# Probabilities of two self attentions turned by VectorE in 32 by 32 blocks

## The chip, the core and the metric

The kernel runs on one core of a Trainium2 chip. A core has five engines, each with an instruction queue of its own that is worked off in order: TensorE (matrix products and transposes, results in PSUM), VectorE, ScalarE, GpSimd and SyncE (here only a queue for DMA). The lines of the profile call them PE, with PEld for its weight loads, then DVE, ACT, POOL and SP. PSUM has 8 banks of 512 fp32 columns by 128 partitions. The metric is the device time of one execution in microseconds; less is better. All data are fp32.

## The reference

Two decoder layers act on x of shape (8 batches, 112 tokens, 512). Each layer is a self attention, a cross attention to a context of 375 rows of 128, and a feed-forward block, each on the layer norm of x and added to x. The two self attentions are what the change touches:

```
layer 0:  32 query heads, 8 key/value heads, width 64
          q, k, v = x@Wq+bq, x@Wk+bk, x@Wv+bv;  q, k rotated by position
          scores  = q.k / 8,  -inf where key > query or query - key >= 64
          probs   = softmax over [scores, sink of the head], sink column dropped
          out     = (probs @ v) @ Wo + bo
layer 1:  16 query heads, 4 key/value heads, width 128
          the same without biases, sinks, with a mask that hides
          nothing at 112 tokens
```

So a query of layer 0 sees the 64 keys up to itself, and a query of layer 1 sees all 112 keys. Layer 1's cross attention (16 heads of width 32, first 112 rows of the context, causal) uses the same softmax helper.

## The kernel before

Tokens lie on partitions where rows are normalised or added (x: seven tiles of 128 tokens), and on columns where they are multiplied (xT: two halves of 448 tokens, four batches each). A self attention (`self_attention`, line 434) has 8 turns: a turn is one group g of four (two key/value heads of layer 0, one of layer 1) and one half hf of the batches. A turn has units: four in layer 0 (a batch with two key/value heads), two in layer 1 (two batches with one key/value head). So every unit is 8 score matrices of 112 by 112.

For a unit, `scores` (line 575) makes the 8 matrices in a PSUM tile "s" of two banks (L583), and `softmax` (line 358) turns them into probabilities: mask added by VectorE in layer 0 (L366), negated row maximum by VectorE (L369), eight exponentials with row sums by ScalarE (L372), the reciprocal by VectorE (L375), and the product with it by GpSimd (L377). In layer 0 GpSimd also copies the sinks into a 113th column (L364). Queries are on the partitions of the result p; the product with v needs keys there. So `contexts` (line 590) begins with `probs_transposed` (line 380): TensorE transposes the 8 matrices, four into one bank of tag "t" (L388), and VectorE copies each bank to pT in SBUF (L389). Then `add` multiplies: v is the stationary operand, four transposed matrices side by side are the 448 moving columns (L599). In layer 0 the two key/value heads of a unit write the partitions 0 to 63 and 64 to 127 of one bank; in layer 1 the two batches write a bank each. ScalarE copies the result to oT (L604).

Around this lie the projections. `prepare(n)` makes keys and queries of turn n (`roped`, line 511): a product on TensorE (pr_k, pr_q), a copy by ScalarE, a DMA from SBUF to SBUF that exchanges halves (L527), a multiplication by VectorE (L530), two operations of GpSimd (L529, L531). `outputs(n, late)` multiplies finished tokens by Wo (po_at) and VectorE adds the result to x (`project_out`, L352). PSUM is shared by three tags of two buffers each: "mm" (projections, values, and po), "s" (scores, two banks each) and "t" (transposes).

TensorE's order is written out by hand. `pipeline` (line 394) gives for every unit: scores of the unit `ahead` (two in layer 0, one in layer 1), the two transposes' steps and `add`; with between=True (layer 0) the transposes come ahead of those scores. `weave` (line 237) spreads the fillers (the next turn's `prepare`, the finished `outputs`) between these steps in proportion to the costs noted beside them; a step marked True wants at least one filler ahead of it. The order of the other engines' queues is set by the framework's planner, from readiness in its own estimate of times and, among the ready, the order of the program. `tc.issue_after` ties some instructions behind another one; `copied` and `spread` hold the last copy and the last product of the softmax for it.

Two further places use these helpers: layer 1's cross attention (lines 1120 to 1249) calls `softmax` and `probs_transposed`, and `cross_attention_0` (line 722) ties the rotation of its context (lines 714 to 718) behind `copied`.

Of the kernel before, what the change touches and what calls it, by code (L numbers as in the profile page):

```python
# [15 lines left out]
P = 128  # L16
# [139 lines left out]
def decoder(ctx: ExitStack, tc: tile.TileContext, i: dict, out: bass.AP):  # L156
# [198 lines left out]
    def completed(hf, late):  # L355
        return [[[0], [1, 2]], [[3, 4], [5, 6]]][hf][late]

    def softmax(pool, ps, mask, sinks, name, bufs=3):

        n = T if sinks is None else T + 1  # L360
        p = pool.tile([T, 8, n], F32, tag="p", bufs=bufs, name=f"p_{name}")
        src = ps[:T, :, :T]
        if sinks is not None:
            nc.gpsimd.tensor_copy(p[:, :, T], sinks)  # L364
        if mask is not None:
            nc.vector.tensor_tensor(p[:, :, :T], src, mask.unsqueeze(1).to_broadcast([T, 8, T]), ALU.add)  # L366
# [10 lines left out]
        spread[:] = [nc.gpsimd.tensor_tensor(p[:, :, :T], p[:, :, :T], total, ALU.mult).ins]  # L377
        return p

    def probs_transposed(pool, p, kept, name):  # L380


        def turn(k):
            if k == 0:
                kept["pT"] = pool.tile([T, 8, T], F32, tag="pT", name=f"pT_{name}")
            pt = turning(f"ppt_{name}_{k}").rearrange("p (h t) -> p h t", h=4)
            for h in range(4):
                nc.tensor.transpose(pt[:T, h, :T], p()[:, 4 * k + h, :T], ident[:T, :T])  # L388
            copied[:] = [nc.vector.tensor_copy(kept["pT"][:, 4 * k : 4 * k + 4, :], pt[:T, :, :T]).ins]  # L389

        return [(0.45, lambda: turn(0)), (0.45, lambda: turn(1))]


    def pipeline(turns, units, ahead, prepare, scores, contexts, outputs, extra, begun=None, finale=None, between=False):

        queue = [(n, u) for n in range(len(turns)) for u in range(units)]  # L400

        def scored(k):
            return [(1.2, lambda: scores(*queue[k]))] if k < len(queue) else []

        def mains(n, us):
            steps = []
            for u in us:
                coming, own = scored(n * units + u + ahead), contexts(n, u)
                if between:
                    steps += own[:2] + coming + own[2:]  # L410
                else:
                    steps += coming + own
            return steps

        if begun is None:
            run(prepare(0) + extra(-1)[:1])
            weave([(1.0, step, True) for k in range(ahead) for _, step in scored(k)], extra(-1)[1:])
        for k in range(begun or (ahead if begun is None else 0), ahead):
            run(scored(k))
        end = len(turns) - 1  # L420
        for n in range(end + (finale is None)):
            filler, late = prepare(n + 1) if n < end else [], outputs(n - 1, True) if n else []
            weave(mains(n, range(units - ahead)), filler + late)
            weave(mains(n, range(units - ahead, units)), outputs(n, False) + extra(n))
        if finale is None:
            run(outputs(end, True))
        else:
            fillers, after = finale(outputs(end - 1, True) + outputs(end, False) + outputs(end, True))
            for u, filler in enumerate(fillers):
                weave(mains(end, [u]), filler)  # L430
            after()


    def self_attention(layer, following=None, behind=None, xT=None):
# [4 lines left out]
        half = width // 2  # L439
        turns = [(g, hf) for g in range(G) for hf in range(2)]  # L440
        held, matrices = [{} for _ in turns], {}

        if l0:
            pool, mid, top, tpool = (
# [29 lines left out]
        v = pool.tile([T, NB, D], F32, tag="v", bufs=1, name=f"v{layer}")  # L474

        oT = None

        def values(b):
            ps = mm(f"pv{layer}_{b}")
# [95 lines left out]
        def scores(n, u):  # L575
            g, hf = turns[n]
            nm = f"{layer}_{g}_{hf}_{u}"
            kT, qT = held[n]["kT"], held[n]["qT"]
            ps = wide(f"ps_{nm}").rearrange("p a (h k) -> p (a h) k", h=4)
            for h in range(4):  # L580
                for k, (b, s) in enumerate(parts(n, u)):
                    at = slice(s * width, (s + 1) * width)
                    nc.tensor.matmul(  # L583
                        ps[:T, 4 * k + h, :T], qT[at, h, bcols(b)], kT[at, bcols(b)], start=True, stop=True
                    )
            held[n]["p", u] = softmax(
                mid, ps, const("mask0", T) if l0 else None, row("sinks")[:, 8 * g : 8 * g + 8] if l0 else None, nm
            )

        def contexts(n, u):  # L590
            g, hf = turns[n]
            nm = f"{layer}_{g}_{hf}_{u}"
            kept = {}

            def add():
                po = [mm(f"po_{nm}_{k}") for k in range(1 if l0 else 2)]
                for k, (b, s) in enumerate(parts(n, u)):
                    at, kv = slice(s * width, (s + 1) * width), g * (P // width) + s
                    nc.tensor.matmul(  # L599
                        po[0 if l0 else k][at, :HT], v[:, b, kv * width : (kv + 1) * width],  # L600
                        kept["pT"][:, 4 * k : 4 * k + 4, :].rearrange("p h q -> p (h q)"), start=True, stop=True,
                    )
# [28 lines left out]
        def go():  # L631
            nonlocal oT, late
            if not l0:
                late = stage_pool("atl1")
                joined.append(following(npool, late))
            oT = (pool if l0 else late).tile([P, 4, NB * T], F32, tag="oT", bufs=1, name=f"oT{layer}")
            pipeline(
                turns, HB if l0 else HB // 2, 2 if l0 else 1, prepare, scores, contexts, outputs, extra,
                begun=None if l0 else 0, finale=finale, between=l0,
            )  # L640
            if l0:
                pool.release()
# [475 lines left out]
    def cross_attention_1(npool, tpool):  # L1118
# [90 lines left out]
        def scores(n, u):  # L1209
            b, nm = n * HB + u // 2, f"e_{n}_{u}"  # L1210
            ps = wide(f"ps_{nm}").rearrange("p a (h k) -> p (a h) k", h=4)
            for c in range(4):
                for k in range(2):
# [250 lines left out]
```

## Time and profile before

| | |
|---|---|
| median of 3 runs | 1901.36 us (1899.02 to 1903.3) |
| profiled execution | 1903.46 us |
| its span, first to last instruction | 1901.5 us |
| mean granted TensorE clock | 0.992 |
| TensorE busy | 1830.2 us (96%), 7088 matmuls |
| VectorE busy | 797.0 us (42%), 1391 instructions |
| ScalarE busy | 660.7 us (35%) |
| GpSimd busy | 585.5 us (31%) |
| stretch 97 to 400 us (seven eighths of layer 0's self attention) | TensorE 289.8, VectorE 174.3, ScalarE 125.2, GpSimd 143.6 of 303 us |
| stretch 1024 to 1166 us (four turns of layer 1's) | TensorE 141.9, VectorE 44.7, ScalarE 41.1, GpSimd 58.6 of 142 us |

How to read the lines: a group has line, engine, operation, the tile written and the tiles read, the shapes (for a matmul contraction * stationary columns, then partitions x moving columns), the count, then busy time in us and the mean of one in ns, then the idle time of the engine just before these instructions and what ended it. An fp32 matrix product is two matmul instructions, so counts are twice those of the code, except for transposes. In a timeline a line is a start, a duration and a run of like instructions; an idle time before it is in brackets. In a table by stretch the bracketed numbers count instructions, and after the busy times of the engines stand the granted clock, the share of the DMA engines and GB/s.

### The profile page before, as it was taken

What the parts mean: (1) busy time and instruction counts of PE and PEld (TensorE: products, weight loads), DVE (VectorE), ACT (ScalarE), POOL (GpSimd) and SP (SyncE); (2) the same over time, 40 slices, a digit from 0 to 9 for tenths busy, and PEclk for the clock granted to TensorE, in tenths of its full rate; (3) what the DMA queues carried; (4) which work ended last, traced back from release to release, by engine and by line L of the source; (5) the groups of instructions that cost most, each with busy time, mean ns of one, the idle gap of its engine ahead of it and who ended that gap; (6) DMA issues with size and microseconds to landing.
All of it is one profiled execution on the core that took longest, in us unless ns stands there. A gap on an engine that the chain in (4) does not pass through costs nothing.

```text
span 1901.5 us, 19724 instructions
## 1 busy us (share of the span) xinstructions
PE 1830.2 (96%) x7088; PEld 986.3 (52%) x7088; DVE 797.0 (42%) x1391; ACT 660.7 (35%) x1948; POOL 585.5 (31%) x512
## 2 busy tenths in 40 slices
PE   7999999899999999989999999999999999999999
PEld 4454544455454455557655555545555444554444
DVE  4455556645454544776532333336722112211213
ACT  3344433444333333375332232236722111121110
POOL 3454544245555540000034334302321111011111
PEclk9999999999999999999999999999999999999999
DMA  6132322243223212011221221301020000000001
GB/s 232 25 113 74 124 75 59 79 141 98 67 78 111 56 39 89 23 67 45 77 63 37 67 77 41 132 4 44 4 107 1 1 0 0 0 0 1 0 0 39
DMA packets 35497, 108.68 MB, mean 57 GB/s; under 512 B 6644, under 2 KB 20012, under 8 KB 28744
## 3 DMA queue, kind: packets, MB, share of 16 engines
q1 hardware_dynamic: 28264, 77.97, 12.7%
q0 software_dynamic: 6848, 29.36, 5.2%
q8 instruction: 56, 0.92, 0.2%
q14 instruction: 41, 0.34, 0.1%
q10 hardware_dynamic: 288, 0.09, 0.0%
HBM read 78.83 MB, written 10.22 MB: 47 GB/s over the span
## 4 chain that ended last, share of the span: by engine, by line
PE 84%; DVE 7%; ACT 5%; DMA 1%; POOL 1%; issue 1%; SPq 1%; ACTq 0%; DVEq 0%; POOLq 0%
PE pf L235 15%; PE po L235 10%; PE po_at L235 9%; PE pr_q L235 8%; PE po_x L235 5%; PE po_x L811 4%; PE pr_k L235 3%; PE pv L235 2%; PE pq_x L235 2%; PE ps L583 2%; PE ph L235 2%; PE po L599 2%; PE ps_x L777 2%; PE po_ff L1051 2%; PE ppt_x L802 2%; PE pk_x L756 2%
## 5 line engine op out<-in xcount | busy, mean ns | idle before, releaser
L235 PE MATMUL pr_q<-xT_at,wq 128*128 128x448 f32 x512 | 205.4, 546 | 2.0 <-ACT raw_q L522 2.0
L235 PE MATMUL po_at<-wo,oT 128*128 128x512 f32 x448 | 205.1, 603 | 0.5 <-ACT oT L604 0.5
L235 PE MATMUL pf<-xT_ff,fup 128*128 128x448 f32 x512 | 199.8, 541 | 1.6 <-ACT xT_ff L313 1.6
L1378 POOL TENSOR_TENSOR h<-silu,h 128x448 f32<-128x448 f32 x64 | 72.9, 1138 | 407.2 <-ACT silu L1377 407.2
L235 PE MATMUL po<-fdn,h 128*128 128x512 f32 x448 | 197.1, 592 | 0.0
L235 PEld LDWEIGHTS pf<-xT_ff,fup 128*128 128x128 f32 x512 | 96.0, 190 | 93.0 <-issue 87.2
L377 POOL TENSOR_TENSOR p<-p,total 112x896 f32<-112x896 f32 x48 | 82.4, 1718 | 192.1 <-DVE total L375 162.3
L235 PEld LDWEIGHTS pr_q<-xT_at,wq 128*128 128x128 f32 x512 | 94.4, 191 | 88.3 <-issue 77.5
L1361 ACT ACTIVATE h<-pf,cols 128x448 f32<-128x448 f32 x64 | 40.5, 633 | 280.5 <-PE pf L235 278.0
L235 PEld LDWEIGHTS po<-fdn,h 128*128 128x128 f32 x448 | 84.6, 190 | 100.7 <-issue 100.1
L372 ACT ACTIVATE p<-p,nmax 112x113 f32<-112x113 f32 x256 | 95.8, 376 | 114.5 <-DVE nmax L369 113.8
L235 PEld LDWEIGHTS po_at<-wo,oT 128*128 128x128 f32 x448 | 82.1, 191 | 94.1 <-issue 86.6
L235 PE MATMUL po_x<-vo,xoT 128*128 128x512 f32 x224 | 102.0, 598 | 0.6 <-ACT xoT L815 0.6
L235 PE MATMUL pf<-h,sw 128*128 128x448 f32 x256 | 101.5, 540 | 0.0
L811 PE MATMUL po_x<-pT_x,kv 125*128 125x448 f32 x192 | 89.3, 548 | 2.7 <-DVE pT_x L806 1.6
L389 DVE COPY pT<-ppt 112x448 f32<-112x448 f32 x96 | 57.3, 614 | 82.2 <-PE ppt L388 82.2
L783 DVE TENSOR_REDUCE nmax_x<-ps_x 112x2 f32<-112x750 f32 x64 | 57.1, 932 | 82.3 <-PE ps_x L777 81.9
L529 POOL TENSOR_TENSOR qT<-raw_q,consts 128x448 f32<-128x448 f32 x64 | 81.2, 1272 | 33.6 <-ACT raw_q L520 18.7
L531 POOL TENSOR_TENSOR qT<-qT,turned_q 128x448 f32<-128x448 f32 x64 | 73.1, 1144 | 58.8 <-DVE turned_q L530 51.1
L934 POOL TENSOR_SCALAR tl<-tr,ternary_bounds 128x512 f32<-128x512 f32 x32 | 51.1, 1596 | 124.6 <-DMA tr<-in_c_w_dram 124.6
L785 ACT ACTIVATE p_x<-ps_x,nmax_x 112x375 f32<-112x375 f32 x124 | 69.7, 574 | 43.9 <-DVE nmax_x L783 43.8
L1391 DVE SCALAR_TENSOR_TENSOR nxt<-po,wr,nxt 128x512 f32<-128x512 f32 x42 | 31.5, 750 | 120.6 <-PE po L235 120.6
(245 smaller groups left out, 3067.6 us busy)
## 6 DMA issues: line engine op xcount, KB each, us to landing
tw<-in_c_w_dram SPq DMA_DIRECT2D x16, 512.0 KB
tr<-in_c_w_dram POOLq DMA_DIRECT2D x32, 256.0 KB, 3.9
signs<-tl POOLq DMA_DIRECT2D x32, 256.0 KB, 2.8
turned_q<-raw_q SPq DMA_DIRECT2D x128, 56.0 KB
turned_q<-raw_q SPq DMA_DIRECT2D x64, 112.0 KB
wq<-in_a_q_dram SPq DMA_DIRECT2D x4, 1024.0 KB
wo<-in_a_o_dram SPq DMA_DIRECT2D x4, 1024.0 KB
bq<-in_b_q_dram SPq DMA_DIRECT2D x4, 1024.0 KB
```

Source lines behind the costliest of these rows:

```text
L235: nc.tensor.matmul(ps, lhsT, rhs, start=(k == 0), stop=(k == len(pairs) - 1))
L372: nc.scalar.activation(p[:, h, :], src[:, h, :], AF.Exp, bias=nmax[:, h : h + 1], accum_out=total[:, h : h + 1])
L377: spread[:] = [nc.gpsimd.tensor_tensor(p[:, :, :T], p[:, :, :T], total, ALU.mult).ins]
L389: copied[:] = [nc.vector.tensor_copy(kept["pT"][:, 4 * k : 4 * k + 4, :], pt[:T, :, :T]).ins]
L529: nc.gpsimd.tensor_tensor(by_batch(dst), by_batch(raw), cos, ALU.mult)
L531: nc.gpsimd.tensor_tensor(dst, dst, turned, ALU.add)
L783: nc.vector.tensor_reduce(nmax, ps[:T, :, :L], AX.X, ALU.max, negate=True)
L785: e = nc.scalar.activation(p[:, 2 * j + s, :], ps[:T, s, :L], AF.Exp, bias=nmax[:, s : s + 1], accum_out=total[:, 2 * j + s : 2 * j + s + 1],)
L811: nc.tensor.matmul(po[0][:, : 4 * T], kv[:, b, c, :], pTs[c], start=(c == 0), stop=(c == NLC - 1))
L934: nc.gpsimd.tensor_scalar(low, w, down[:, m : m + 1], None, ALU.is_lt)
L1361: nc.scalar.activation(at["h1"][:, c, hf * HT : (hf + 1) * HT], ps[:, :HT], AF.Identity, bias=bias)
L1378: nc.gpsimd.tensor_tensor(at["h3"][:, c, tokens], s, at["h1"][:, c, tokens], ALU.mult)
```

## The change

The 8 matrices of a unit are no longer transposed by TensorE. VectorE transposes them from p to pT in blocks of 32 by 32, one instruction for a pair of key block and query block and for all eight heads (32 partitions, 8 x 32 elements). Layer 0 transposes the 9 of 16 block pairs in which the mask leaves a key visible, layer 1 all 16. pT now has keys on partitions and [query block, head, query in block] on columns, and the rest of it is set to zero once in layer 0. p is kept in two tiles of 128 by 8 by 128 per layer, set to zero once, in place of three of 112 by 8 by 113 or 112; pT in two tiles of 128 by 1024.

The transposes of a unit are called one unit ahead: after a unit's `add` comes `turn`, which transposes the next unit. The value product of four heads is made in two parts, the first three query blocks (384 columns) and the last 16 queries (64 columns), with the same v. Its result lies in tag "t" instead of "mm". `between` is gone: scores of the coming unit always come ahead of the own `add`. Layer 1's cross attention keeps its transposes by TensorE; its p tiles have rows of 128 elements, and alternate between two pools of two buffers in place of three and one.

```diff
-    def softmax(pool, ps, mask, sinks, name, bufs=3):
-        n = T if sinks is None else T + 1
-        p = pool.tile([T, 8, n], F32, tag="p", bufs=bufs, name=f"p_{name}")
+    def softmax(p, ps, mask, sinks, name):
...
+    class Probabilities:
+        def __init__(self, pool, bufs, name):
+            self.name = name
+            self.p = [pool.tile([P, 8, P], F32, tag="p", bufs=bufs, name=f"p_{name}_{k}") for k in range(bufs)]
+            for t in self.p:
+                nc.gpsimd.memset(t, 0.0)
+            self.pT, self.ready, self.filled, self.turned = [], {}, 0, 0
+
+        def turned_into(self, pool):
+            self.pT = [pool.tile([P, 4, 256], F32, tag="pT", name=f"pT_{self.name}_{k}") for k in range(2)]
+            return self.pT
+
+        def softmax(self, ps, mask, sinks, name):
+            p = self.p[self.filled % len(self.p)]
+            self.filled += 1
+            softmax(p[:T, :, : T if sinks is None else T + 1], ps, mask, sinks, name)
+
+        def turn(self, keys, key):
+            p, pT = self.p[self.turned % len(self.p)], self.pT[self.turned % 2]
+            self.turned += 1
+            for q, (lo, hi) in enumerate(keys):
+                for k in range(lo, hi):
+                    last = nc.vector.transpose(
+                        pT[32 * k : 32 * k + 32, q, :].rearrange("p (h q) -> p h q", h=8),
+                        p[32 * q : 32 * q + 32, :, 32 * k : 32 * k + 32],
+                    )
+            copied[:] = [last.ins]
+            self.ready[key] = pT
...
-                coming, own = scored(n * units + u + ahead), contexts(n, u)
-                if between:
-                    steps += own[:2] + coming + own[2:]
-                else:
-                    steps += coming + own
+                steps += scored(n * units + u + ahead) + contexts(n, u)
...
+        if opened:
+            opened()
...
+        probs = Probabilities(mid, 2, f"at{layer}")
+        if l0:
+            for t in probs.turned_into(late):
+                nc.gpsimd.memset(t, 0.0)
...
+        def turn(n, u):
+            n, u = divmod(n * units + u + 1, units)
+            if n < len(turns):
+                probs.turn([(0, 1), (0, 2), (0, 3), (1, 4)] if l0 else [(0, 4)] * 4, (n, u))
...
-                po = [mm(f"po_{nm}_{k}") for k in range(1 if l0 else 2)]
+                po = [turning(f"po_{nm}_{k}") for k in range(1 if l0 else 2)]
+                pT = probs.ready[n, u]
                 for k, (b, s) in enumerate(parts(n, u)):
                     at, kv = slice(s * width, (s + 1) * width), g * (P // width) + s
+                    vs, heads = v[:, b, kv * width : (kv + 1) * width], slice(4 * k * 32, (4 * k + 4) * 32)
+                    to = po[0 if l0 else k][at, :HT].rearrange("p (h q) -> p h q", h=4)
                     nc.tensor.matmul(
-                        po[0 if l0 else k][at, :HT], v[:, b, kv * width : (kv + 1) * width],
-                        kept["pT"][:, 4 * k : 4 * k + 4, :].rearrange("p h q -> p (h q)"), start=True, stop=True,
+                        to[:, :, :96].rearrange("p h (i q) -> p i h q", i=3), vs,
+                        pT[:T, :3, heads].rearrange("p i (h q) -> p i h q", h=4), start=True, stop=True,
+                    )
+                    nc.tensor.matmul(
+                        to[:, :, 96:], vs, pT[:T, 3, heads].rearrange("p (h q) -> p h q", h=4)[:, :, : T - 96],
+                        start=True, stop=True,
                     )
...
-            return probs_transposed(late, lambda: held[n]["p", u], kept, nm) + [(0.8 if l0 else 1.5, add, True)]
+            return [(0.8 if l0 else 1.5, add, True), (0.0, lambda: turn(n, u))]
...
-            last = u % 4 == 3
-            held[n]["p", u] = softmax(pool if last else ppool, ps, const("mask1", T), None, nm, 1 if last else 3)
+            p = (pool if u % 2 else ppool).tile([P, 8, P], F32, tag="p", bufs=2, name=f"p_{nm}")[:T, :, :T]
+            held[n]["p", u] = p
+            softmax(p, ps, const("mask1", T), None, nm)
```

More of the change, by code (lines that the diff above doesn't have):

```diff
@@ L377, in softmax @@
         spread[:] = [nc.gpsimd.tensor_tensor(p[:, :, :T], p[:, :, :T], total, ALU.mult).ins]
-        return p
     def probs_transposed(pool, p, kept, name):
@@ L384, in turn @@
             if k == 0:
-                kept["pT"] = pool.tile([T, 8, T], F32, tag="pT", name=f"pT_{name}")
+                kept["pT"] = pool.tile([P, 4, 256], F32, tag="pT", name=f"pT_{name}").rearrange("p a b -> p (a b)")[
+                    :T, : 8 * T
+                ].rearrange("p (h t) -> p h t", h=8)
             pt = turning(f"ppt_{name}_{k}").rearrange("p (h t) -> p h t", h=4)
@@ L391, in probs_transposed, with pipeline @@
         return [(0.45, lambda: turn(0)), (0.45, lambda: turn(1))]
-    def pipeline(turns, units, ahead, prepare, scores, contexts, outputs, extra, begun=None, finale=None, between=False):
+    class Probabilities:
[23 more added lines that the diff above has]
+            self.ready[key] = pT
+    def pipeline(turns, units, ahead, prepare, scores, contexts, outputs, extra, begun=None, finale=None, opened=None):
         queue = [(n, u) for n in range(len(turns)) for u in range(units)]
@@ L441, in self_attention @@
         held, matrices = [{} for _ in turns], {}
+        units = HB if l0 else HB // 2
         if l0:
@@ L585, in scores @@
                     )
-            held[n]["p", u] = softmax(
-                mid, ps, const("mask0", T) if l0 else None, row("sinks")[:, 8 * g : 8 * g + 8] if l0 else None, nm
-            )
+            probs.softmax(
+                ps, const("mask0", T) if l0 else None, row("sinks")[:, 8 * g : 8 * g + 8] if l0 else None, nm
+            )
+        def turn(n, u):
+            n, u = divmod(n * units + u + 1, units)
+            if n < len(turns):
+                probs.turn([(0, 1), (0, 2), (0, 3), (1, 4)] if l0 else [(0, 4)] * 4, (n, u))
         def contexts(n, u):
@@ L592, in contexts @@
             nm = f"{layer}_{g}_{hf}_{u}"
-            kept = {}
             def add():
-                po = [mm(f"po_{nm}_{k}") for k in range(1 if l0 else 2)]
+                po = [turning(f"po_{nm}_{k}") for k in range(1 if l0 else 2)]
+                pT = probs.ready[n, u]
                 for k, (b, s) in enumerate(parts(n, u)):
                     at, kv = slice(s * width, (s + 1) * width), g * (P // width) + s
+                    vs, heads = v[:, b, kv * width : (kv + 1) * width], slice(4 * k * 32, (4 * k + 4) * 32)
+                    to = po[0 if l0 else k][at, :HT].rearrange("p (h q) -> p h q", h=4)
                     nc.tensor.matmul(
-                        po[0 if l0 else k][at, :HT], v[:, b, kv * width : (kv + 1) * width],
-                        kept["pT"][:, 4 * k : 4 * k + 4, :].rearrange("p h q -> p (h q)"), start=True, stop=True,
+                        to[:, :, :96].rearrange("p h (i q) -> p i h q", i=3), vs,
[4 more added lines that the diff above has]
+                        start=True, stop=True,
                     )
@@ L634, in go @@
                 late = stage_pool("atl1")
+                probs.turned_into(late)
                 joined.append(following(npool, late))
@@ L637, in go @@
             pipeline(
-                turns, HB if l0 else HB // 2, 2 if l0 else 1, prepare, scores, contexts, outputs, extra,
-                begun=None if l0 else 0, finale=finale, between=l0,
+                turns, units, 2 if l0 else 1, prepare, scores, contexts, outputs, extra,
+                begun=None if l0 else 0, finale=finale, opened=lambda: turn(0, -1),
             )
```

## The prediction

> **What bounds the kernel now.** I read the page's 40 slices first, then the groups, then busy time by stretch, then TensorE and VectorE in order of time.
>
> ```profile
> PE   7999999899999999989999999999999999999999
> DVE  4455556645454544776532333336722112211213
> PEclk9999999999999999999999999999999999999999
> ```
>
> TensorE is busy in nearly every slice, VectorE never above 7. A slice is 47.5 us: layer 0's self attention is slices 1 to 8, layer 1's about 21 to 26. So the end is set by TensorE, and time taken from it is gained as long as nothing else takes its place. The groups of the changed lines:
>
> ```profile
> L388 PE MATMUL ppt<-consts,p 112*112 112x112 f32 x384 | 49.7, 264 | 8.0 <-POOL p L377 7.5 <-ACT kvT L849 0.6
> L599 PE MATMUL po<-pT,v 112*64 112x448 f32 (+1 forms) x192 | 61.6, 564 | 0.8 <-ACT raw_q L522 0.6
> L389 DVE COPY pT<-ppt 112x448 f32<-112x448 f32 x96 | 57.3, 614 | 82.2 <-PE ppt L388 82.2
> L675 DVE COPY rk<-pB x4: 409/424/424, 373.7 to 668.1; 128x256 f32<-128x256 f32 x4
> ```
>
> The first three are what goes or is cut; the fourth is the only VectorE row with 256 elements per partition, the size of a new transpose. By stretch (TensorE, its weight loads, VectorE, ScalarE, GpSimd busy, then the clock), five stretches of layer 0 and two of layer 1:
>
> ```profile
> 97.00:138.00 41.00, 41.00 (x188) 20.65 (x187) 24.11 (x33) 16.84 (x72) 24.43 (x22) 1.00 0.40 132
> 178.00:220.00 42.00, 42.00 (x184) 21.04 (x182) 24.07 (x33) 17.03 (x75) 19.50 (x18) 0.96 0.38 128
> 220.00:261.00 41.00, 38.52 (x183) 20.09 (x182) 23.57 (x33) 17.81 (x77) 19.55 (x18) 0.98 0.26 80
> 306.00:350.00 44.00, 39.59 (x181) 19.96 (x179) 29.40 (x49) 15.09 (x59) 22.68 (x18) 0.96 0.32 110
> 350.00:400.00 50.00, 46.63 (x227) 26.45 (x228) 28.12 (x56) 22.58 (x73) 16.79 (x13) 0.97 0.16 54
> 1061.00:1095.00 34.00, 33.98 (x127) 18.52 (x126) 10.82 (x16) 10.26 (x41) 14.62 (x12) 1.00 0.16 34
> 1095.00:1132.00 37.00, 36.97 (x130) 19.55 (x129) 11.38 (x17) 10.26 (x41) 14.63 (x12) 1.00 0.29 88
> ```
>
> A turn has four units in layer 0 and two in layer 1. VectorE is at 58% in layer 0 and at 31% in layer 1: the same change meets a loaded engine in one and an idle one in the other.
>
> **TensorE, removed.** Eight transposes a unit:
>
> ```profile
> 207.30 0.93 PE L388 MATMUL ppt<-consts,p 112*112 112x112 f32 x8
> 208.16 1.04 PE L583 MATMUL ps<-kT,qT 64*112 64x112 f32 x16
> 212.76 0.97 PE L599 MATMUL po<-pT,v 112*64 112x448 f32 x4
> 213.66 0.98 PE L388 MATMUL ppt<-consts,p 112*112 112x112 f32 x8
> 1070.86 0.55 PE L388 MATMUL ppt<-consts,p 112*112 112x112 f32 x4
> 1071.24 3.19 PE L235 MATMUL pr_q<-xT_at,wq 128*128 128x448 f32 x8
> ```
>
> From the start to the next group's start it is 0.86 us (layer 0), and 0.38 for four in layer 1. With 0.9 and 0.78 a unit: 32 x 0.9 + 16 x 0.78 = **41.3 us** less.
>
> **TensorE, added.** Each value product becomes one of 384 and one of 64 columns, each in two passes. The streaming is the same; what is new are weight loads. In layer 1 (weights 128 wide) a 64-column pass is like the pR row, 15.4 us / 128 = 0.12 us; it streamed as 64/448 of 0.376 = 0.054 before. 4 x 0.066 x 16 = **+4.2 us**. In layer 0 the two products lie in two column halves of the array and now run side by side: four passes take 212.76 to 213.66, 0.90 us, against 1.68 for layer 1's four. The new order puts all four passes of one half ahead of the other's. [...] The gate products are the row for it, eight passes in one half, then eight in the other:
>
> ```profile
> 1415.41 0.89 PE L235 MATMUL pgate<-wg,xT_ff 128*64 128x8 f32 x16
> ```
>
> Within one half they start 58 ns apart, so sixteen in line would take 15 x 58 = 870 ns from first start to last; the trace has 689, and the second half begins at 1415.67, before the first half's sixth. I take +0.1 us a unit, **+3.2**; ends 0 and +22. Net: TensorE's need falls by 34 us.
>
> **VectorE.** Removed: two copies a unit. Two in a row take 1.15 us, so one costs 0.53 there. Added: 9 transposes a unit in layer 0, 16 in layer 1; none is in the trace. Of 256 elements, the L675 row says 0.42 us alone. Back to back, copies of 448 start 0.08 us earlier than their duration (0.53 against 0.61), which gives 0.34. [...]
>
> Layer 1: 16 x 0.42 - 2 x 0.53 = +5.7 us a unit, 11 + 11.4 = 22 of 33 us a turn. Covered: VectorE idles there, and the value product comes at least 20 us after its scores while softmax (6 us from 1061.6 to 1067.6) and transposes (6.7) need 13. Were that cover gone the 6.7 would show per unit. One loss: at the stage's opening the block of 6.7 us lies beside the evacuation of the values (L484), I allow 2 us. Gain 12.5 - 4.2 - 2 = **6 us**.
>
> Layer 0, stretch 97 to 400 (28 units): VectorE needs 174.3 - 56 x 0.53 + 28 x 9 x 0.42 = **250 us** (174.3 is the sum of the seven stretches, 289.8 TensorE's); TensorE 289.8 - 28 x 0.8 = 267, of which some 6 are clock lost after the two stalls below. So VectorE rises to 95% of TensorE's need, above it where the context's rotation and the layer norms join (306 to 400). In order behind the transposes stand mask add and maximum, the evacuation x<-x,po_at (TensorE's next projection waits for its bank) and turned_q (GpSimd's qT, and so the scores). There are also only two probability buffers: the mask add two units on waits for the transposes.
>
> What speaks for the change there is the order. Before, the next turn's first transposes waited for GpSimd:
>
> ```profile
> 260.15 1.00 PE L388 MATMUL ppt<-consts,p 112*112 112x112 f32 x4 [2.48 <-POOL p L377]
> ```
>
> and the clock then fell to 0.5 and 0.71 for 4 us each, 3.2 us more; the same at 177.6. Now scores, a key and a query projection (6.4 us) precede the value product, and the transposes take 9 x 0.42 = 3.8 of these. I don't count the whole 11 us, as VectorE is late more often. Of the 42 us between 303 and 261 I take a third, since at 303 us VectorE would be at 83% and at 261 at 96%: stage at 289, gain **14 us**; ends 0 and 42. The first four units add 4 x 0.8 = **3**.
>
> Moved: po from the banks "mm" to "t", which leaves projections alone on "mm" (L599 waited 0.8 us in all: nothing). GpSimd's memsets, six tiles at most, lie at each stage's head where it idles (0 if covered; some 2.6 us each if not, twice its 128x512 row of 1.3 us). No DMA is added or moved.
>
> **Sum.** 14 + 3 + 6 = 23 us. The profiled execution took 1903.5 (span 1901.5), which gives 1880; the median of the runs is 2 us lower, so **1879 us**.
>
> **Rivals.**
> *VectorE keeps up (0.13).* Transposes at 0.34: 230 us in the stretch, 88% of 261. Stage near 272: 31 + 3 + 8 = 42, 1860 us. For it: list order can put evacuations first. [...]
> *Layer 0 gives nothing back (0.19).* VectorE becomes its bound, each stall also costs clock: 303 stays, layer 1's 6 remain: 1895 us.
> [...]
> *Slower (0.25): the transpose is dear.* One mechanism, at L0's VectorE: need 144.6 + 252 t, t being its duration. It decides where this passes 303 + 9, at t = 0.66; at 0.69 it is 319, with 5% idle 335: 32 - 6 = 26 us slower, 1927. For it: no such instruction in the trace. [...]
>
> **How the numbers follow.** My case has 0.38, own range 1868 to 1890. A difference of 0.2% (3.8 us) is what this kernel's runs can tell. Faster: 0.38 + 0.13, 0.17 of the second rival and 0.01 of the third, 0.69. Same: 0.02 + 0.03 = 0.05. Slower: 0.25 + 0.01 = 0.26. The range from 1853 to 1912 leaves out most of the last rival and little else.
>
> **What would show it.** Transposes near 0.42 us, 288 in layer 0 and 256 in layer 1, no L388 in the self attentions; VectorE at 85% in layer 0 and 60% in layer 1; layer 1's turns about 1 us shorter, layer 0's some 2; value passes of layer 0 in pairs. I am wrong if transposes last 0.6 or more, if TensorE waits for pT or evacuations over 30 us in layer 0, or if the halves don't overlap.

## The result and the profile after

The changed kernel takes 1926.31 us (median of 6 runs, 1921.12 to 1931.17), against 1898.98 us (1895.07 to 1903.3) for the kernel before on the same chip: a ratio of 1.0141, 95% interval 1.0119 to 1.0162. It is 27 us **slower**; 1879 us had been predicted. The profiled execution took 1921.12 us (span 1919.3), at the lower end of its runs, while that of before lay at the upper end of its own, so the two traces differ by 18 us only. Sizes by stage are read from single executions, one for each kernel; layer 0's stage alone ended between 392.0 and 396.5 us in kernels that do the same there.

The 40 slices of the page, TensorE, VectorE and the granted clock:

```profile
PE   7888888899999999989989999999999999999999
DVE  4677777965354544686555566656722112211113
PEclk9999999999999999999999999999999999999999
```

In layer 0 (slices 1 to 8) TensorE is at 8 in seven of eight slices, where it was at 9 in six. VectorE has risen to 7 in most of them and to 9 in one: it isn't full, and yet TensorE waits. The groups of the changed lines:

```profile
L418 DVE STREAM_TRANSPOSE pT_at<-p_at 32x256 f32<-32x256 f32 x544 | 237.0, 436 | 68.7 <-POOL p_at L375 59.9 <-PE po L647 0.3
L643 PE MATMUL po<-pT_at,v 112*64 112x384 f32 (+1 forms) x192 | 57.6, 514 | 1.9 <-DVE pT_at L418 1.9
L647 PE MATMUL po<-pT_at,v 112*64 112x64 f32 (+1 forms) x192 | 21.0, 232 | 0.0
```

The new transposes take 436 ns each, and TensorE hardly ever waits for their result (1.9 us in all, idle time before L643). So the loss is neither in the price of a transpose nor in the product that uses it. Busy time by stretch (TensorE, weight loads, VectorE, ScalarE, GpSimd, clock): four turns of layer 0, two of layer 1, then 97 to 380 us of layer 0.

```profile
101.40:149.10 47.70, 40.72 (x171) 19.84 (x169) 35.13 (x55) 18.50 (x82) 23.22 (x21) 0.93 0.34 113
190.40:236.90 46.50, 39.94 (x173) 19.45 (x169) 37.00 (x66) 18.42 (x83) 21.71 (x19) 0.96 0.35 116
236.90:279.00 42.10, 36.64 (x163) 18.25 (x161) 31.74 (x57) 15.49 (x64) 18.90 (x17) 0.92 0.25 78
279.00:327.80 48.80, 41.34 (x180) 20.42 (x179) 35.74 (x73) 20.25 (x90) 21.71 (x19) 0.97 0.22 56
1040.40:1075.90 35.50, 35.50 (x124) 19.32 (x123) 19.80 (x40) 10.26 (x41) 14.91 (x12) 1.00 0.31 93
1075.90:1110.30 34.40, 32.18 (x114) 17.58 (x113) 19.77 (x39) 10.16 (x41) 15.14 (x12) 1.00 0.16 34
97.00:380.00 283.00, 244.16 (x1054) 120.21 (x1054) 223.74 (x404) 108.08 (x462) 128.51 (x114) 0.95 0.28 88
```

The six turns of layer 0 from 52.8 to 327.8 us take 41 to 49 us; before, the six from 53.7 to 306.4 took 40 to 46. In the last row TensorE is idle for 38.8 us and VectorE busy for 79%. The same stretch before, with TensorE idle for 12.7 us:

```profile
97.00:380.00 283.00, 270.32 (x1230) 138.54 (x1229) 166.34 (x254) 118.76 (x491) 132.74 (x116) 0.97 0.28 88
```

TensorE's largest waits there, each with its sum, how often, and the longest one, first before the change, then with it:

```profile
PE ppt L388 <- POOL p L377: 6.9, 3, 2.6
PE pr_q L235 <- ACT raw_q L522: 2.0, 1, 2.0
```

```profile
PE ps L618 <- POOL qT L566: 14.8, 7, 3.8
PE po_at L235 <- ACT raw_q L557: 13.6, 6, 3.4
PE pr_q L235 <- ACT raw_q L557: 3.8, 2, 1.9
PE pr_q L235 <- ACT raw_k L557: 3.6, 2, 2.6
```

None of the four names VectorE. How VectorE can stand behind such waits shows in order of time, here 20 us of layer 0 (a start, a duration, a run of like instructions, in brackets the idle time before it):

```profile
161.07 0.88 DVE L418 STREAM_TRANSPOSE pT_at<-p_at 32x256 f32<-32x256 f32 x2 [1.80 <-POOL p_at L375]
...
162.63 3.13 DVE L418 STREAM_TRANSPOSE pT_at<-p_at 32x256 f32<-32x256 f32 x7
...
166.34 1.08 DVE L364 TENSOR_TENSOR p_at<-ps,consts 112x896 f32<-112x896 f32 x1
...
167.88 1.08 DVE L367 TENSOR_REDUCE nmax<-p_at 112x8 f32<-112x904 f32 x1
...
169.05 0.39 ACT L370 ACTIVATE p_at<-p_at,nmax 112x113 f32<-112x113 f32 x1 [5.83 <-DVE nmax L367]
...
172.05 0.61 ACT L557 ACTIVATE raw_q<-pr_q,cols 128x448 f32<-128x448 f32 x1
...
172.71 3.70 PE L235 MATMUL po_at<-wo,oT 128*128 128x512 f32 x8 [1.69 <-ACT raw_q L557]
...
174.33 4.05 DVE L418 STREAM_TRANSPOSE pT_at<-p_at 32x256 f32<-32x256 f32 x9 [1.40 <-POOL p_at L375]
...
179.02 0.62 DVE L565 TENSOR_TENSOR turned_q<-turned_q,consts 128x448 f32<-128x448 f32 x1
179.77 1.13 POOL L566 TENSOR_TENSOR qT<-qT,turned_q 128x448 f32<-128x448 f32 x1 [1.13 <-DVE turned_q L565]
180.95 0.45 PE L618 MATMUL ps<-kT,qT 64*112 64x112 f32 x4 [3.76 <-POOL qT L566]
```

Two chains run through it. **The first**: VectorE waits 1.80 us for p, transposes until 165.8, and only then adds the mask to scores that TensorE had ready since 163.5. Mask and maximum come about 3 us later than they could, ScalarE's eight exponentials wait for them, and behind these, in ScalarE's queue, stands the copy of a query projection that TensorE had finished at 166.7. It comes at 172.05, so the PSUM bank is late and TensorE waits 1.69 us. **The second**: nine transposes (after another idle 1.40 us) stand in front of `turned_q`; GpSimd's qT waits for it, and the scores for that, 3.76 us. In layer 1 the first chain is the larger one:

```profile
1071.91 4.92 DVE L418 STREAM_TRANSPOSE pT_at<-p_at 32x256 f32<-32x256 f32 x11 [1.79 <-POOL p_at L375]
...
1077.58 2.26 DVE L418 STREAM_TRANSPOSE pT_at<-p_at 32x256 f32<-32x256 f32 x5
...
1079.88 1.09 DVE L367 TENSOR_REDUCE nmax<-ps 112x8 f32<-112x896 f32 x1
1081.00 0.35 ACT L370 ACTIVATE p_at<-ps,nmax 112x112 f32<-112x112 f32 x1 [9.47 <-DVE nmax L367]
...
1083.65 0.57 ACT L555 COPY raw_k<-pr_k 128x448 f32<-128x448 f32 x1
...
1084.27 1.02 PE L235 MATMUL pr_q<-xT_at,wq 128*128 128x448 f32 x2 [2.22 <-ACT raw_k L555]
```

VectorE is busy for little more than half of these turns, but when the scores are ready (1076.0) it is in the middle of sixteen transposes. The maximum comes 4 us later, and TensorE pays 2.22 of them. From 985 to 1240 us TensorE is busy for 243.26 us, against 254.81 before, so it is idle for 11.7 us where 0.2 were. The largest wait there is this one:

```profile
PE pr_q L235 <- ACT raw_k L555: 6.7, 3, 2.2
```

The next ones are 2.8 us for a copy of the values, which stood behind the first sixteen transposes of the stage, and 2.5 us for qT.

### The profile page after: what moved, and what is told of

The parts are those of the page before. It is cut to its first block, busy times and chain, and to the rows that moved or that the text cites. A ratio compares the mean times of both kernels' runs of the same rounds, so it can differ in the third digit from the quotient of the medians.

```text
span 1919.3 us, 19770 instructions
## 1 busy us (share of the span) xinstructions
PE 1808.3 (94%) x6896; PEld 972.4 (51%) x6896; DVE 971.5 (51%) x1839; ACT 655.1 (34%) x1946; POOL 590.1 (31%) x518
## 5 line engine op out<-in xcount | busy, mean ns | idle before, releaser
L418 DVE STREAM_TRANSPOSE pT_at<-p_at 32x256 f32<-32x256 f32 x544 | 237.0, 436 | 68.7 <-POOL p_at L375 59.9
L235 PE MATMUL po_at<-wo,oT 128*128 128x512 f32 x448 | 216.0, 630 | 13.6 <-ACT raw_q L557 13.6
L1428 POOL TENSOR_TENSOR h<-silu,h 128x448 f32<-128x448 f32 x64 | 72.8, 1138 | 407.2 <-ACT silu L1427 407.1
L370 ACT ACTIVATE p_at<-p_at,nmax 112x113 f32<-112x113 f32 x256 | 95.9, 377 | 172.2 <-DVE nmax L367 172.1
L375 POOL TENSOR_TENSOR p_at<-p_at,total 112x896 f32<-112x896 f32 x48 | 82.3, 1715 | 208.9 <-DVE total L373 208.8
L235 PEld LDWEIGHTS po_at<-wo,oT 128*128 128x128 f32 x448 | 86.9, 201 | 112.4 <-issue 96.6
L566 POOL TENSOR_TENSOR qT<-qT,turned_q 128x448 f32<-128x448 f32 x64 | 77.9, 1222 | 50.6 <-DVE turned_q L565 39.1
L1441 DVE SCALAR_TENSOR_TENSOR x<-po,wr,x 128x512 f32<-128x512 f32 x42 | 31.5, 751 | 118.8 <-PE po L235 118.8
L618 PE MATMUL ps<-kT,qT 64*112 64x112 f32 (+1 forms) x768 | 65.2, 272 | 22.4 <-POOL qT L566 22.4
```

Of the source, the lines that this page charges most:

```text
L235: nc.tensor.matmul(ps, lhsT, rhs, start=(k == 0), stop=(k == len(pairs) - 1))
L370: nc.scalar.activation(p[:, h, :], src[:, h, :], AF.Exp, bias=nmax[:, h : h + 1], accum_out=total[:, h : h + 1])
L418: last = nc.vector.transpose(pT[32 * k : 32 * k + 32, q, :].rearrange("p (h q) -> p h q", h=8), p[32 * q : 32 * q + 32, :, 32 * k : 32 * k ...
L566: nc.gpsimd.tensor_tensor(dst, dst, turned, ALU.add)
L618: nc.tensor.matmul(ps[:T, 4 * k + h, :T], qT[at, h, bcols(b)], kT[at, bcols(b)], start=True, stop=True)
L1428: nc.gpsimd.tensor_tensor(at["h3"][:, c, tokens], s, at["h1"][:, c, tokens], ALU.mult)
```

## The experiments

The table has all of them: the median, the ratio to the kernel before (run on the same chip), then from the trace the start of layer 0's cross attention ("L0 ends") and the time from the start of the last product of layer 0's feed-forward block to the first scores of layer 1's cross attention ("L1 takes").

| kernel | median us | ratio, 95% | L0 ends | L1 takes |
|---|---|---|---|---|
| before | 1898.98 | | 396.5 | 308.1 |
| the change | 1926.31 | 1.0141 (1.0119 to 1.0162) | 411.7 | 316.1 |
| change in layer 0 alone | 1913.53 | 1.0084 (1.0061 to 1.0106) | 410.3 | 308.0 |
| change in layer 1 alone | 1909.35 | 1.0050 (1.0032 to 1.0069) | 396.0 | 318.1 |
| three p tiles | 1933.7 | 1.0192 (1.0168 to 1.0215) | 417.2 | 317.9 |
| one transpose a unit | 1865.06 | 0.9818 (0.9795 to 0.9842) | 372.0 | 295.7 |
| 6 of 9, 8 of 16 transposes | 1884.58 | 0.9926 (0.9898 to 0.9953) | 389.3 | 300.8 |
| exponentials without mask, maximum | 1903.37 | 1.0025 (1.0017 to 1.0034) | 390.6 | 318.2 |
| ... and VectorE off the scores | 1885.21 | 0.9922 (0.9907 to 0.9936) | 384.0 | 303.7 |
| the same in the kernel before | 1885.66 | 0.9932 (0.9914 to 0.9949) | 383.9 | 308.1 |
| ... and queries without sines | 1888.99 | 0.9950 (0.9931 to 0.9969) | 389.4 | 302.1 |
| ... no mask, no maximum at all | 1867.4 | 0.9831 (0.9814 to 0.9847) | 370.0 | 299.8 |
| change, maxima first | 1907.39 | 1.0044 (1.0032 to 1.0056) | 407.1 | 309.8 |
| layer 1 alone, split 10 and 6 | 1899.35 | 1.0002 (0.9992 to 1.0012) | 395.2 | 309.8 |
| layer 1 alone, split where late | 1889.32 | 0.9947 (0.9930 to 0.9964) | 393.9 | 299.9 |
| layer 1 alone, two units ahead | 1907.68 | 1.0053 (1.0033 to 1.0073) | 392.0 | 320.2 |
| before, layer 1 two units ahead | 1907.62 | 1.0049 (1.0036 to 1.0061) | 394.4 | 315.3 |

### Where: one layer at a time, and the number of tiles

The change was put under a switch `by_vector`, true in one layer; the other keeps the functions of the kernel before.

```diff
+        by_vector = l0            # or: not l0
-            return [(0.8 if l0 else 1.5, add, True), (0.0, lambda: turn(n, u))]
+            if not by_vector:
+                return old_contexts(n, u, nm)
+            return [(0.8 if l0 else 1.5, add, True), (0.0, lambda: turn(n, u))]
```

> The change in layer 0 alone; layer 1's self attention transposes on TensorE as before (layer 1's cross attention has its former p tiles too). In the trace of the changed kernel layer 0's self attention ended 15 us later, the two stages behind it took back 4, layer 1's lost 8. If the two layers lose each for itself: 11 to 15 us slower than before, about 1912, and layer 0's stage ends near 412. If layer 1's loss only follows from layer 0's: as slow as the whole change, about 1926.

> The change in layer 1 alone; layer 0's self attention transposes on TensorE, with three p tiles and its former order. If each layer loses for itself: 7 to 10 us slower than before, about 1907, with waits of some 2 us for the projections' bank in every turn of layer 1. My forecast's sum for layer 1 (6 us gained) would give 1893.

Measured: 15.2 us lost by layer 0 alone, 11.1 by layer 1 alone, 26.3 together against 27.3 for both. **Each layer loses for itself.** Layer 1's loss is thus no echo of layer 0's; my forecast had the wrong sign in both.

```diff
-        probs = Probabilities(mid, 2, f"at{layer}")
+        probs = Probabilities(mid, 3, f"at{layer}")
```

> The change with three probability tiles per layer in place of two (a narrower p tile in layer 1's cross attention makes room). Theory of the buffers: mask add, exponentials and GpSimd's copy of the sinks wait for the transposes of the unit two before because p has two buffers (GpSimd's sink copy waited 73 us for transposes in layer 0); with three, layer 0 gets back 10 us or more: 1910 to 1916. Theory of the queue: the mask add and the maximum stand behind the transposes on VectorE whatever the number of tiles, and ScalarE's copies of the projections stand behind the exponentials: no more than 3 us back, 1923 to 1929.

It is 7 us slower still than the change, outside both ranges of the expectation: the two tiles are not the cause. VectorE does its work in nearly the same order with three. What the further 7 us are, some 5 of them in layer 0, was not followed up.

### How much: fewer transposes

```diff
-                for k in range(lo, hi):
+                for k in range(hi - 1 if q == 3 else hi, hi):     # one transpose a unit
...
                 for k in range(lo, hi):
+                    if (q + k) % 2 ...:                           # the second kernel
+                        continue
```

> The changed kernel with one transpose per unit (the last) in place of 9 and 16; the rest of pT is zero, so its value products work on other numbers. Tiles, order of the matrix products, column parts and banks stay. If VectorE's time in the transposes makes the loss, by whatever route: TensorE's net 34 us come through, some 1865 to 1880, and layer 0's stage ends before 385. If the new order of the matrix products, the column parts, the banks or the two tiles make it: above 1905.

> Only 6 of 9 transposes in layer 0 and 8 of 16 in layer 1 (320 in place of 544; the other blocks of pT are zero, so its values are others). Between one transpose a unit (48 in all, 1865) and all (1926): if each transpose costs the same, as a delay in a queue does, 1865 + 61 x 272/496 = 1898. If VectorE has slack that the first ones fill without harm, and only the last ones hurt: 1872 to 1885.

With one transpose a unit the kernel gains 33 us. The new order of the matrix products, the column parts, the banks and the tiles are all still in it, so none of them shows a cost (VectorE is also freed of its copies here: 152.6 us busy from 97 to 380, 166.3 before), and TensorE's net 34 us of my sum are there to be had. That pT is mostly zero did not help by the clock: it is 0.97 in that stretch, as before the change. All 61 us between this kernel and the change are the 496 further transposes. They don't cost alike: the step from 48 to 320 of them costs 19.5 us (0.07 each), the step from 320 to 544 costs 41.7 (0.19 each), while VectorE is busy for 0.436 with each. So VectorE hides most of them, and hides the last ones worst; my two expectations for the middle (1898, or 1872 to 1885) are decided for the second, at its edge.

### How: the links cut one by one

The exponentials were given a zero as bias and the scores as input, so that nobody in the self attentions uses VectorE's mask additions and maxima (the line as it runs there):

```diff
-                p[:, h, :], src[:, h, :], AF.Exp, bias=nmax[:, h : h + 1], accum_out=total[:, h : h + 1]
+                p[:, h, :T], ps[:T, h, :T], AF.Exp, bias=zero[:T], accum_out=total[:, h : h + 1]
```

> All 544 transposes as in the change, and VectorE does the same mask additions and maxima, but nobody in the two self attentions waits for them: the exponentials read the scores in PSUM with a zero as bias, so mask and maximum are left out of the probabilities (masked sums go to a tile of their own; layer 1's cross attention keeps a narrower p tile). Theory of the chain (transposes hold up mask add and maximum, these the exponentials, these ScalarE's copies of the projections, these TensorE): more than half of the 61 us between the change and the kernel with one transpose come back, 1870 to 1895, and TensorE's waits for raw_q and raw_k copies go. If the loss comes by VectorE's throughput, or by turned_q and qT behind the transposes: 1910 or more.

Less than half came back, 1903 us, between the two ranges, and in layer 1 nothing. The waits show why (first layer 0 from 40 to 411 us, then layer 1 from 985 to 1262):

```profile
ACT p_at L373 <- DVE free_at L367: 146.3, 32, 10.3
```

```profile
ACT p_at L373 <- DVE nmax L370: 119.8, 14, 10.1
```

The exponentials use nothing of what VectorE makes, but both read the same PSUM tile, and in the program as built they still wait for VectorE's reading of it. The link was not cut in layer 1, and only shortened in layer 0 (by the maximum). The next kernel lets VectorE do the same instructions on a tile in SBUF, and queues them behind the latest transpose (or, in the control, behind the latest copy of transposes):

```diff
-            nc.vector.tensor_tensor(masked[:, :, :T], src, mask..., ALU.add)
+            with tc.issue_after(copied[0]) ...:         # the same for the maximum
+                nc.vector.tensor_tensor(masked[:, :, :T], masked[:, :, :T], mask..., ALU.add)
...
+        elif free is not None:
+            src = free[:T, :, :T]           # what the maximum reads
```

> As the run before that took mask and maximum out of the exponentials' way, but VectorE's mask additions and maxima now read a tile of their own in SBUF and not the scores: in that run the exponentials still waited for VectorE's instruction on the same PSUM tile (146 us in layer 0, 120 in layer 1), so the link had not been cut. Same instructions and sizes on VectorE, all 544 transposes. Mask and maximum are left out of the probabilities. Theory of the chain: most of the 61 us come back, 1870 to 1890, layer 0's stage ends at 372 to 385 and layer 1's takes 296 to 303 us. If VectorE's load or turned_q behind the transposes makes most of the loss: 1900 or more.

> The control: the kernel before, transposes on TensorE, with the exponentials freed from VectorE in the same way (mask and maximum left out of the probabilities, VectorE does them on other tiles). TensorE has little idle time to lose in the kernel before, so if the link matters only because of the transposes: 1890 to 1899. If the link costs as much without them: 1860 to 1880.

Now the exponentials wait for TensorE, and no projection waits for ScalarE in layer 0 for more than 0.7 us in all:

```profile
ACT p_at L377 <- PE ps L628: 61.8, 22, 9.0
...
PE ps L628 <- POOL qT L576: 15.4, 11, 2.9
```

41 us came back, but the control is needed to read it: the kernel before gains 15 us from the same cut, 12.6 of them in layer 0, a size that neither range of its expectation had. **In layer 1** the control is worth nothing (308.1 us both times) and the change with the cut takes 303.7 instead of 316.1 (296 to 303 had been expected): 12.4 us came back with the first chain. **In layer 0** the change costs 15.2 us with the link (411.7 against 396.5) and 0.1 without it (384.0 against 383.9). So with the first chain cut the change no longer loses in layer 0, and TensorE's waits for the copies of raw_q and raw_k there fall from 24 us to 0.7. The cut is not a pure one, for the order of VectorE's and GpSimd's queues in this kernel differs from that of the change in more than this link. And the first chain does not explain why TensorE's saving there (24.5 us: 396.5 to 372.0) isn't gained. For this the second chain was cut too, in layer 0: VectorE's product with the sines goes to a tile nobody reads.

```diff
-            nc.vector.tensor_tensor(by_batch(turned), by_batch(turned), sin, ALU.mult)
+            aside = top.tile([P, HT], F32, tag="aside", bufs=1, name=f"aside_{name}") if l0 else turned
+            nc.vector.tensor_tensor(by_batch(aside), by_batch(turned), sin, ALU.mult)
```

> As the run in which VectorE no longer touched the scores, and in layer 0 the second link is cut too: VectorE's product with the sines goes to a tile of its own, and GpSimd adds what the DMA brought, so keys and queries wait for the DMA and not for VectorE (mask, maximum and, in layer 0, the sines are left out of the result; VectorE's work is the same). If the queries behind the transposes are the rest of layer 0's loss: its stage ends at 372 to 377 (384 with the first link alone, 372 with one transpose a unit), 1872 to 1878 in all, and the waits of the scores for qT (15 us) go. If VectorE's load hurts by another route: 1883 or more.

My expectation failed: layer 0 ended 5 us later, and the scores waited for qT for 20.3 us in place of 15.4. This cut didn't test what it was meant to, for the queries remained late: qT stands in GpSimd's queue behind work that waits for VectorE by other ways (from 40 to 390 us, 96.7 us for the reciprocals and 52.7 for transposes that free p). And VectorE had become fuller in these kernels. The groups of the kernel with the first cut:

```profile
L368 DVE TENSOR_TENSOR free_at<-free_at,consts 112x896 f32<-112x896 f32 x30 | 41.1, 1370 | 0.9
L575 DVE TENSOR_TENSOR turned_q<-turned_q,consts 128x448 f32<-128x448 f32 x28 | 34.2, 1224 | 4.1 <-POOL p_at L383 2.7 <-DMA turned_q<-raw_q 1.1
```

(in the change these took 1082 and 774 ns). The last kernel of this row tells load from order; it leaves the mask additions and maxima away, links cut as in the kernel with VectorE off the scores.

> All 544 transposes; VectorE makes no mask additions and no maxima in the two self attentions, the exponentials wait for the scores alone (mask and maximum are left out of the probabilities). VectorE's busy time in the stretch 97 to 380 us falls from 253 to about 180 of 283. If what kept TensorE's saving from coming through in layer 0 is VectorE's load: its stage ends at 360 to 368 (control without the change 383.9, less 24), 1860 to 1872 in all, and the scores wait less than 5 us for qT. If it is the block of nine transposes in front of the queries' sine products whatever the load: 376 to 384 and 1876 to 1885.

The two kernels from 97 to 380 us, first with mask additions and maxima on other tiles, then without any:

```profile
97.00:380.00 283.00, 262.94 (x1174) 134.62 (x1173) 253.43 (x443) 113.71 (x490) 158.90 (x124) 0.95 0.30 93
```

```profile
97.00:380.00 283.00, 269.71 (x1212) 139.23 (x1211) 212.47 (x398) 118.39 (x487) 142.19 (x131) 0.97 0.33 108
```

VectorE falls from 90% to 75% (I had expected 64%), the stage ends at 370.0, and the waits for qT fall from 15.4 to 5.8 us. The whole time, 1867 us, is in the range for the load; the stage's end and the waits lie between the two, nearer to the load's. Of the 24 us, 14 come with the load taken off VectorE. No control of this last kernel was run; the kernel before with the first cut has TensorE idle for only 5.3 of the 283 us, so it could gain little of them without the change. About 10 us stay open: TensorE is idle for 13.3 us here, 5.8 of them for qT. With the cut, then, layer 0 comes near VectorE's throughput, as the forecast had it; without it, VectorE stands at 79% and the order has already cost more.

### Other orders

If the order makes the loss, another one should give it back. First, scores of layer 1 two units ahead, so that every maximum precedes the transposes, and the control without the change:

```diff
-                turns, units, 2 if l0 else 1, prepare, scores, contexts, outputs, extra,
+                turns, units, 2, prepare, scores, contexts, outputs, extra,
...
+            if ahead == units:
+                run(filler + late + mains(n, [0]))
+                weave(mains(n, [1]), outputs(n, False) + extra(n))
+                continue
```

> The change in layer 1 alone, and there the scores run two units ahead in place of one, with all projections of the next turn ahead of the two units of a turn. So each maximum comes before the transposes on VectorE, and a projection's copy no longer meets exponentials that wait. If layer 1's loss (11 us with the change alone) is this order and not the transposes' time itself: its gain of 8 us comes through, 1886 to 1894. If VectorE's transposes are too long in any order: 1905 or more.

> The kernel before with nothing but that order in layer 1 (scores two units ahead, the next turn's projections first), transposes on TensorE. It is the control of the run with the change in layer 1 and this order. The order takes nothing from TensorE: 1896 to 1904.

Both are 9 us slower than before and equal to each other, where a gain and no change had been expected: this order has a price of its own, and the change gains nothing in it (in the kernel with it TensorE waits for oT, v and x, 13 us in all). It is not a way out.

Second, only VectorE's order. `issue_after` queues an instruction behind another one of its engine, without a wait. Layer 0: all nine transposes behind the latest maximum. Layer 1: ten transposes as before, six after the next maximum.

```diff
+                if l0:
+                    with tc.issue_after(maxima[0]):
+                        probs.turn(keys, (n, u))
+                else:
+                    probs.turn(keys, (n, u), range(10))
+        def turn_rest(n, u):            # called after the next scores, ahead of add
+            with tc.issue_after(maxima[0]):
+                probs.turn([(0, 4)] * 4, (n, u), range(10, 99))
```

> The change with another order on VectorE alone. Layer 0: a unit's nine transposes are queued behind the maximum of the unit after it. Layer 1: the first ten of sixteen stay, the last six are queued behind the maximum of the next scores, ahead of the value product. Nothing waits for more than before, no work is added. If the order (maximum behind transposes) makes the loss: layer 0's stage ends before 400 (411.7 with the change), layer 1's takes 300 to 308 us (316 with the change), 1893 to 1908 in all. If the transposes' time hurts in any order: 1918 or more.

> The change in layer 1 alone, with ten of its sixteen transposes as in the change and six behind the maximum of the next scores; layer 0 as before. If the order makes layer 1's loss: the waits of 2.2 us for the copies of keys go and TensorE's 8 us are gained, 1890 to 1898. If not: 1905 to 1912, as with the change in layer 1 alone.

Layer 1 got back 6 to 8 us, layer 0 only 4.6 (407.1, not below 400), short of what I expected. The medians say more than these traces: 18.9 us lie between the change and the first of these kernels, 10 us between their two profiled executions, so layer 0 may have got back more than 4.6. With the maxima first, the transposes are late instead. TensorE's waits in layer 0 of the first of these kernels:

```profile
PE po L654 <- DVE pT_at L419: 8.7, 4, 5.3
...
PE ps L619 <- POOL qT L567: 6.4, 5, 1.8
PE po L658 <- DVE pT_at L419: 4.4, 4, 2.3
```

In layer 1 alone the split kernel is level with before, just short of the expected 1890 to 1898. Two late places are left in its trace:

```profile
PE pr_q L235 <- ACT raw_k L561: 5.0, 2, 2.5
PE pev L1233 <- DVE ev L1234: 4.1, 1, 4.1
```

A maximum behind ten transposes (4.5 us) in some turns, and the next stage's first values behind the last unit's ten. Only these were moved:

```diff
+        def early(n, u):
+            return 4 if u == 0 else 2 if n == 7 else 10
-            with tc.issue_after(maxima[0]):
-                probs.turn([(0, 4)] * 4, (n, u), range(10, 99))
+            with tc.issue_after(late_values[1] if (n, u) == (7, 1) else maxima[0]):
+                probs.turn([(0, 4)] * 4, (n, u), range(early(n, u), 99))
...
-                nc.vector.tensor_copy(v[:, b % HB, :], ps[:T, :])
+                late_values.append(nc.vector.tensor_copy(v[:, b % HB, :], ps[:T, :]).ins)
```

> The change in layer 1 alone, split as before, with three numbers changed: of a turn's first unit only four of sixteen transposes come ahead of the maximum (ten so far: its maximum was at 1090.6 us, and two key copies came 2.5 us late), of the very last unit two, and its others behind two copies of the next stage's values (which came 4.1 us late). If these places are what keeps the gain back: 1887 to 1894, faster than before. If not: 1897 to 1901, as with the former split.

1889.32 us, 0.9947 of before (0.9930 to 0.9964): **faster than both kernels**. Both waits are gone, what is left is short (the largest two of TensorE from 985 to 1262 us):

```profile
PE po L685 <- DVE pT_at L419: 1.2, 1, 1.2
PE po L689 <- DVE pT_at L419: 1.1, 2, 0.8
```

Layer 1 takes 299.9 us in this trace, 8.2 less than before; the medians differ by 11. My sum has 16 x 0.78 - 4.2 = 8.3 for TensorE in this layer, but the agreement is luck: with one transpose a unit the layer gained 12.4. It is the same engine, with the same sixteen transposes of 0.436 us and the same number of tiles as in the kernel that lost 11 us; only their place in VectorE's queue differs. A split of this kind was not tried in layer 0.

## Why the prediction was wrong, point by point

- **TensorE, removed: right; added: too much in layer 1.** Net 34 us were summed, 33 measured with one transpose a unit. By layer the sum has 25.6 and 8.3 us, that kernel's trace 24.5 and 12.4. The 4.2 us added in layer 1 are not there: a unit's value products take 1.68 us from their start to the next group's (1087.38 to 1089.06), as before (1074.27 to 1075.95). In layer 0 no run shows the 22 us at the upper end of what was added: a unit's value product takes 0.91 us from its start to the next group's (229.45 to 230.36), 0.90 before, and the row of the gate products had pointed the right way.
- **VectorE, the price of a transpose: right.** 0.436 us; 0.42, the time of a copy of 256 elements that stands alone, had been taken. Nine in a row take 4.05 us, 0.45 each, so they don't overlap as the copies of 448 did; the value worked out from those (0.34) would have misled. No run shows the 0.69 us that the rival on the slower side is worked out with, nor any transpose of 0.66 or more (the longest of the 544 took 0.443), so that rival had the right sign by a wrong mechanism.
- **Layer 1, "covered: VectorE idles there": this step failed.** I asked whether the transposes are done before their own value product needs them, and they are. I didn't ask who else queues behind them. 11 us of VectorE's work a turn were covered, and yet a maximum behind sixteen transposes made TensorE wait up to 2.2 us, 6.7 in all, the largest part of the 11.7 us that it is idle from 985 to 1240: 8 to 11 us lost instead of 6 gained. (The 2 us allowed for the values at the stage's opening were 2.8.) The same transposes in another place of the queue gained.
- **Layer 0, the stage as a balance of busy times: this step failed.** I set VectorE's 250 us against TensorE's 267, found both below 303 and took a third of the 42 us between 303 and 261 as gain: 17 us with the stage's opening, where 15 were lost. I had named the very instructions that stand behind the transposes (mask add and maximum, turned_q and so the scores), but their lateness counted only as gain not had, never as time lost against before. In the trace TensorE's waits for their results are 35.8 us in 97 to 380 (the sum of the four rows), against 2.0 for the same results before. My own sign, over 30 us of waits for pT or evacuations in layer 0, did not come as I had put it: these are 26 us in the whole stage. The sign left out qT, another 17.
- **The gap before the first transposes of a turn would vanish: right, but replaced.** TensorE's waits for p, 6.9 us in 97 to 380, are gone; VectorE now waits for the same p (26 us there) with everything behind it waiting too.
- **Two probability buffers: named, and not the cause.** Three gave nothing.
- **The clock** was granted at 0.95 in 97 to 380 us, at 0.97 before. My estimate of its part is 0.02 of 283 us, about 6 us; no run separates it from the idle times.

## What to carry to other kernels

Moving work to an engine that is half idle is not free even if its result is early: list what stands behind the new block in that engine's queue, follow each of these to the bottleneck engine, and price the block's length as lateness there, above all where a third engine has copies behind the late instruction. Busy shares don't show this. If the block can be cut, place it by hand: the short instruction that others wait for first, the long block behind it, and only as much ahead as fits before the input of the short one arrives.

## What the runs showed of the hardware

- VectorE's transposes are not slowed by GpSimd: 0.436 us (359 of them, no GpSimd product beside) and 0.435 (172, over half of their time beside one). VectorE's sine products, which read two SBUF tiles, take 0.62 us alone (43 of 80), 1.09 on average and up to 3.9 where GpSimd's products overlap more than half of them (29; all counted in the trace of the change). The mask add took 1082 ns on average in the change, with the scores in PSUM as one input, and 1370 with both inputs in SBUF, in the kernel with VectorE off the scores; the same cut in the kernel before took it from 1087 to 1320. So this cut made VectorE's work dearer, which blurs the kernels with VectorE off the scores.
- In the program as built, of two engines that only read the same PSUM tile one waits for the other (the exponentials for VectorE, 146 and 120 us). The wait went when the second reader left the tile.
